# A graph layer's edge stage on one core: the batch's signal moves from a matmul to a drain of TensorE's sequencer

## Chip, core and metric

The kernel runs on 1 core of one Trainium2 chip. The metric is the device time of one execution in microseconds (us); lower is better. Before the change: 4782.93 us, the median of 3 runs (4782.77 to 4783.48). All data is float32, indices are int32.

## What is computed

One layer of a graph network with a residual: 12,500 nodes of 160 numbers (64 scalars and 32 vectors of three) and 400,000 edges sorted by their target node `dst`. Cut to what matters:

```python
h = maximum(layernorm(x), 0)                       # per node
y0 = h[:, :64] @ W_l1_0 * a / 8                    # a: one number per node
y1 = einsum('nuc,uv->nvc', h[:, 64:].reshape(n, 32, 3), W_l1_1) * a / sqrt(32)
s0, s1 = the same with W_sc0, W_sc1
w = silu(e16 @ fc_W1 / 4) @ fc_W2 / 8              # per edge: 16 -> 64 -> 192
w_a, w_b, w_c, w_d = split(w, [64, 64, 32, 32])
ys0, ys1 = y0[src], y1[src]                        # gather
mid0 = concat[w_a * ys0 * e0, w_d * (ys1 . e1) / sqrt(3)]
mid1 = concat[(w_b * ys0)[:, :, None] * e1, (w_c * e0)[:, :, None] * ys1]
z0, z1 = scatter-add of mid0, mid1 by dst, / sqrt(10)
out = x + sin(pi/8) * [s0, s1] + cos(pi/8) * [z0 @ W_l2_0, z1 @ W_l2_1] * a / sqrt(96)
```

`e0` and `e1` are the first and the other three of four numbers per edge.

## The kernel before

**Node stage** (to about 220 us). Layer norm, both linear maps, and the table `y_d` (one row of 160 numbers per node) written to DRAM.

**Edge stage.** 3125 tiles of 128 edges, in batches of four tiles: 782 batches, the last with one tile. The stage is one Python loop over `b`, fully unrolled, in an order written out by hand: under `manual_schedule` TensorE, VectorE and ScalarE run what the loop emits in the order in which it emits it. Step `b` of the loop emits, in this order:

- `weigh(b + 2)` (L574 to L584): four matmuls at L582 (eight instructions on TensorE, as each float32 matmul runs as two) turn the hidden layer `hT` into the batch's 192 edge weights per edge, in one of two PSUM tiles `pw`; then ScalarE copies three numbers per edge into the same tile (L583). The next matmuls into a `pw` tile wait until VectorE has made the products of the batch two earlier.
- `name_rows(b + 10)` (L545): ScalarE copies the batch's gather indices, `ids`.
- What earlier steps left for ScalarE (`leaving`): `hT` from the hidden matmul (L571), sums out of PSUM (`zs` L629, `za` L641, `os` L654 and L655).
- `lift_rows(b + 2)` (L493): ScalarE scales the four gathered rows of 160 by `e0`.
- `dots_of(b + 1)` (L498 to L501) and `products(b + 1)` (L505, L506, L509, L510) on VectorE, which read `pw`, the gathered rows `yg` and the lifted rows. L510 is the last reader of `pw`. Every third step `select` (L600) makes the one-hot matrices of the next three batches from the target indices.
- `load(b + 10)` (L555): GpSimd issues four indirect DMAs, one for each tile, that gather rows of `y_d` by `src`. Nine `yg` buffers lie between this and its use. 22 of the batches do not gather: their rows are made on the spot out of kept rows of `x` ("made" rows: transposes at L709 and matmuls at L720 to L722 on TensorE, 88 times each).
- `accumulate` (L665, L668): VectorE adds a finished group of nodes into the result.
- `sums(b)` (L623): four matmuls (eight instructions) multiply the one-hot matrices with the products and add them up in PSUM tile `pz` over the tiles of a group of nodes; at a group's end `turn` (three transposes, L637) and `map_sums` (three matmuls, L650) follow a few steps later.
- On even steps `hidden` (L566): one matmul (two instructions) into `px`, the hidden layer of the batches ahead.

SyncE loads edge features `xe` (L277) ten batches ahead, each load waiting for the matmuls that read its buffer before.

**Signals of TensorE.** TensorE signals on one semaphore, and in each batch the last weights matmul does it, for all matmuls since the signal before. In the built program 781 of the 782 batches have this signal; 99 hidden matmuls, 80 of the sums, 16 transposes and 4 maps of the stage signal as well. ScalarE waits for the batch's signal before L583, in an instruction of its sequencer that also waits for VectorE. What ScalarE reads from PSUM later in the step was finished before the weights and needs no wait of its own. VectorE's L498 waits for L583 (ScalarE's semaphore) and for the batch's gathers, and through L583 for the weights.

Of the kernel before, what the change touches and what calls it, by code (L numbers as in the profile page):

```python
# [18 lines left out]
P = 128  # L19
M0 = 64  # L20
M1 = 32
D = M0 + 3 * M1
FC_IN = 16
FC_H = 64
NW = 2 * M0 + 2 * M1
# [5 lines left out]
TG = 12  # L31
# [14 lines left out]
def kernel(  # L46
# [19 lines left out]
    nc = tc.nc  # L66
    N = x.shape[0]
    NT = attr.shape[1]
# [49 lines left out]
    ident = const.tile([P, P], F32, name="ident")  # L118
# [93 lines left out]
    wn0 = const.tile([P, 2, M0], F32, name="wn0")  # L212
    wn1 = const.tile([P, 2, 3 * M1], F32, name="wn1")

    w1 = const.tile([P, 2 * FC_H], F32, name="w1")
    w2 = const.tile([P, NW], F32, name="w2")

    wo = const.tile([P, 3, D], F32, name="wo")
    wc = const.tile([P, 3, D], F32, name="wc")
# [70 lines left out]
    a_sb = const.tile([P, NT], F32, name="a_sb")  # L290
# [23 lines left out]
    with (  # L314
# [129 lines left out]
        with tc.manual_schedule(engines=engines):  # L444
# [11 lines left out]
            last = len(steps) - 1  # L456
# [57 lines left out]
    with (  # L514
# [13 lines left out]
        pxs = [banks.tile([P, 512], F32, name=f"px{i}") for i in range(2)]  # L528
        turns = {"px": 0}

        def next_px():
            turns["px"] += 1
            return pxs[turns["px"] % 2]
# [4 lines left out]
        def tiles_of(b):  # L538
            return list(range(b * GT, min((b + 1) * GT, T)))
# [20 lines left out]
        def hidden(s):  # L560

            if 2 * s < NB:
                xe = blocks[s * 2 * GT // BT]
                r = slice(32 * (s % 4), 32 * (s % 4 + 1))
                ph = next_px()
                nc.tensor.matmul(ph, w1[r, :], xe[r, :], start=True, stop=True)  # L566
                leaving.append(lambda: activate(s, ph))

        def activate(s, ph):
            hT = hid.tile([P, 512], F32, name="hT")  # L570
            nc.scalar.activation(hT, ph, AF.Silu, scale=1.0 / math.sqrt(FC_IN))  # L571
            hids[s] = hT

        def weigh(b):  # L574
            hT = hids[b // 2]
            pw = pws[b % 2]
            n = len(tiles_of(b))
            for k in (0, 2, 1, 3):
                if k < n:
                    r = slice(FC_H * (k // 2), FC_H * (k // 2 + 1))  # L580
                    o = P * (b % 2 * 2 + k % 2)
                    nc.tensor.matmul(pw[:, k, 0:NW], hT[r, o:o + P], w2[r, :], start=True, stop=True)  # L582
            nc.scalar.activation(pw[:, :n, NW:NW + 3], e4_of(b)[:, :n, 1:4], AF.Copy)  # L583
            wts[b] = pw  # L584

# [4 lines left out]
        def e4_of(b):  # L590
            g, k = divmod(b, K)
            o = g % EG * TG + k * GT
            return raws[g // EG][:, o:o + GT, :]
# [22 lines left out]
        def sums(b):  # L616
            pr = prs.pop(b)
            for k, t in enumerate(tiles_of(b)):
                g = group_at[t]
                first, last = t == starts[g], t == ends[g] - 1  # L620
                if first:
                    z_ps[g] = pzs[g % 2][:, 0:ZC]
                nc.tensor.matmul(z_ps[g], sels[t // TG][:, t % TG, :], pr[:, k, :], start=first, stop=last)  # L623
                if last:
                    leaving.append(lambda g=g: z_out(g))

        def z_out(g):
            zs = post.tile([P, ZC], F32, name="zs")
            nc.scalar.activation(zs, z_ps.pop(g), AF.Copy)  # L629
            z_sb[g] = zs  # L630

        def turn(g):

            zs = z_sb.pop(g)
            pt = pzs[g % 2][:, 0:3 * P].rearrange("p (k c) -> p k c", k=3)
            for k in range(3):
                nc.tensor.transpose(pt[:, k, :], zs[:, P * k:P * (k + 1)], ident)  # L637

            def out_of():
                za = post.tile([P, 3, P], F32, name="za")  # L640
                nc.scalar.activation(za, pt, AF.Copy)  # L641
                zT[g] = za
            leaving.append(out_of)

        def map_sums(g):

            za = zT.pop(g)
            px = next_px()
            for k, lo, hi in ((0, 0, 96), (2, 96, D), (1, M0, D)):
                nc.tensor.matmul(px[:, lo:hi], za[:, k, :], wc[:, k, lo:hi], start=k == 0, stop=k == 1)  # L650

            def out_of():
                os = post.tile([P, 1, D], F32, name="os")
                nc.scalar.activation(os[:, 0, 0:M0], px[:, 0:M0], AF.Copy)  # L654
                nc.scalar.activation(os[:, 0, M0:].rearrange("p (u c) -> p c u", c=3),  # L655
                                     px[:, M0:D].rearrange("p (c u) -> p c u", c=3), AF.Copy)
                o_sb[g] = os
            leaving.append(out_of)
# [46 lines left out]
        def made_turn(r, k):  # L705
            hm, oh = turned.pop((r, k))
            pt = next_px()[:, 0:3 * P].rearrange("p (k c) -> p k c", k=3)
            for i, v in enumerate((hm[:, 0:P], hm[:, LO:D], oh)):
                nc.tensor.transpose(pt[:, i, :], v, ident)  # L709

            def out_of():
                tm = mk.tile([P, 3, P], F32, name="m_t")
                nc.scalar.activation(tm, pt, AF.Copy)
                turned[r, k] = tm
            leaving.append(out_of)

        def made_map(r, k):
            tm = turned.pop((r, k))
            po = next_px()
            nc.tensor.matmul(po[:, 0:M0], tm[:, 0, :], wn0[:, 0, :], start=True, stop=True)  # L720
            nc.tensor.matmul(po[:, M0:D], tm[:, 1, :], wn1[:, 0, :], start=True, stop=True)
            nc.tensor.matmul(po[:, D:D + NT], tm[:, 2, :], a_sb, start=True, stop=True)  # L722

            def out_of():
                pm = mk.tile([P, D + NT], F32, name="m_p")
                nc.scalar.activation(pm, po[:, 0:D + NT], AF.Copy)
                mapped[r, k] = pm
            leaving.append(out_of)
# [13 lines left out]
        def plan(r):  # L742

            b = made_at[r]
            step, lag = (6, 2) if b * GT <= wide else (12, 6)
            end = b - 7 - lag
            last = end - (end + 1) % 6
            first = last - step * (GT - 1)
            for when, b, f in ([(at_start, first - 6, made_load), (on_vector, first - 3, made_moments),
                                (on_vector, first - 1, made_reciprocal)]):  # L750
                when.setdefault(max(b, 0), []).append(lambda f=f: f(r))
            for k in range(GT):
                j = first + step * k
                for when, b, f in ((on_vector, j - 1, made_rows), (on_tensor, j, made_turn), (on_tensor, j + lag, made_map),
                                   (on_vector, j + lag + 2, made_attr), (on_scalar, j + lag + 3, made_leave)):
                    when.setdefault(b, []).append(lambda f=f, k=k: f(r, k))
# [15 lines left out]
        with order:  # L772
# [6 lines left out]
            for s in range(3):  # L779
                hidden(s)  # L780
                all_leave()
# [4 lines left out]
            for b in range(min(2, NB)):  # L786
                weigh(b)
                lift_rows(b)
# [7 lines left out]
            for g, e in enumerate(last_batch):  # L796
                at_end = e + 4 >= NB
                t = e + (1 if at_end else 2)
# [4 lines left out]
            for b in range(NB + 3):  # L803
                u, k = divmod(b, K)
# [3 lines left out]
                if b < NB:  # L808
                    q, r = divmod(b, EG * K)
# [6 lines left out]
                if b + 2 < NB:  # L816
                    weigh(b + 2)
# [17 lines left out]
                if b < NB:  # L835
                    sums(b)
                for g in turns_at.get(b, []):
                    turn(g)
                for g in maps_at.get(b, []):
                    map_sums(g)  # L840
                if b % 2 == 0:
                    hidden((b + 6) // 2)
# [5 lines left out]
    with (  # L848
# [11 lines left out]
        with tc.For_i(0, n, 1) as _:  # L860
# [4 lines left out]
            with tc.For_i(0, TP // GT, 1) as g:  # L865
                xe = fp.tile([FC_IN, 512], F32, name="f_xe")
# [30 lines left out]
                pr = fp.tile([P, GT, ZC], F32, name="f_pr")  # L897
# [3 lines left out]
                for k in range(GT):  # L901
# [16 lines left out]
                    zs = fp.tile([P, ZC], F32, name="f_zs")  # L918
# [4 lines left out]
            with tc.For_i(0, NT, 1) as i:  # L923
                zt = fp.tile([P, ZC], F32, name="f_zt")
                nc.sync.dma_start(zt, z_d[ds(i * P, P), :])
                pt = fpp.tile([P, 3, P], F32, name="f_pt")
# [4 lines left out]
                po = fpp.tile([P, D], F32, name="f_po")  # L931
# [50 lines left out]
```

## Time and profile before

| | |
|---|---|
| median of 3 runs | 4782.93 us |
| the profiled execution's own time | 4772.01 us |
| its span (first to last instruction) | 4770.2 us |
| mean granted TensorE clock | 0.904 |
| VectorE busy | 3410.0 us (71%) |
| GpSimd busy | 2967.2 us (62%) |
| ScalarE busy | 1819.5 us (38%) |

How to read it: all numbers on the profile come from the one profiled execution. PE is TensorE's matmuls, PEld its weight loads, DVE VectorE, ACT ScalarE, POOL GpSimd, SP SyncE; a "q" behind an engine is its sequencer, which waits, signals and issues DMAs and is not counted as busy. A matmul's end is modelled by the profile, its start is recorded. In a view by time a row is: start (us), duration (us), engine, line, operation, out<-in, shapes, how many were merged, and in brackets the engine's idle time before it and what ended that. A row of the waits is: engine, its tile and line <- what it waited for: us in total, times, longest. In the view of one line a row is: engine, operation, count: shortest/median/longest ns, first and last start in us. "issue" and "remote" are waits whose end the profile cannot put down to an engine.

### The profile page before, as it was taken

The numbers are of one execution on the slowest core, as the hardware profiler recorded it, in microseconds if no ns is written. First come the engines' busy times: TensorE is split into PE (matmuls) and PEld (weight loads), VectorE is DVE, ScalarE is ACT, GpSimd is POOL, SyncE is SP. The second block draws the span as 40 slices with busy tenths as digits, with TensorE's granted clock in tenths as the row PEclk, the third lists the DMA queues.
The fourth block names the chain that finished last, engine by engine and source line by source line (L and its number), as shares of the span: only waits on it lengthen the run. The fifth ranks groups of instructions, "written<-read, shape, count | busy, mean of one in ns | idle before, by whom it ended". The sixth has DMA issues, their size and how long they took to land.

```text
span 4770.2 us, 55691 instructions
## 1 busy us (share of the span) xinstructions
PE 4061.2 (85%) x16329; PEld 2320.6 (49%) x16329; DVE 3410.0 (71%) x7531; ACT 1819.5 (38%) x6330; POOL 2967.2 (62%) x3137
## 2 busy tenths in 40 slices
PE   3568988888888888888888888998988889889988
PEld 3434554444454445444444445555545445555544
DVE  4547777777777777777777767777777777777766
ACT  3423334333343333333433333333333434343333
POOL 4466666666666666666666666666666666666663
PEclk7779899899999998999998899898989998898988
DMA  5422222222222222222222222222222222232222
GB/s 175 136 61 65 65 67 66 61 65 65 67 66 65 67 65 63 64 65 68 67 64 68 63 63 63 64 66 62 67 62 63 66 63 68 62 105 63 62 61 61
DMA packets 227725, 333.87 MB, mean 70 GB/s; under 512 B 54714, under 2 KB 171526, under 8 KB 227158
## 3 DMA queue, kind: packets, MB, share of 16 engines
q0 software_dynamic: 150000, 256.20, 21.8%
q1 hardware_dynamic: 63618, 65.63, 4.4%
q10 hardware_dynamic: 13796, 8.44, 0.6%
q8 instruction: 129, 2.11, 0.2%
q14 instruction: 182, 1.49, 0.1%
HBM read 306.83 MB, written 23.22 MB: 69 GB/s over the span
## 4 chain that ended last, share of the span: by engine, by line
PE 25%; another core or an unknown queue 23%; issue 22%; DVE 18%; ACT 10%; DMA 1%; ACTq 0%; DVEq 0%; POOL 0%; SPq 0%; POOLq 0%
PE pz L623 15%; PE pw L582 6%; ACT yge L493 5%; DVE pr L506 3%; DVE tmp L498 3%; DVE tmp L501 2%; PE px L566 2%; DVE pr L510 2%; DVE pr L509 2%; DVE both L500 2%; ACT pw L583 1%; DVE pr L505 1%; DVE sel L600 1%; ACT hT L571 1%
## 5 line engine op out<-in xcount | busy, mean ns | idle before, releaser
L555 POOL DMA_INDIRECT yg<-y_d,ids x2997 | 2842.2, 948 | 1612.5 <-issue 782.1
L623 PE MATMUL pz<-pr,sel 128*128 128x384 f32 x6250 | 2529.9, 549 | 143.5 <-issue 83.9
L623 PEld LDWEIGHTS pz<-pr,sel 128*128 128x128 f32 x6250 | 1253.0, 211 | 1130.3 <-issue 550.7
L498 DVE TENSOR_TENSOR tmp<-yg,pw 128x384 f32<-128x384 f32 x760 | 416.7, 548 | 1147.5 <-ACT pw L583 1084.6
L583 ACT ACTIVATE pw<-raw 128x12 f32<-128x12 f32 x782 | 139.8, 179 | 2802.8 <-issue 1190.0
L582 PE MATMUL pw<-w,hT 64*128 64x192 f32 x6250 | 825.8, 368 | 388.6 <-DVE pr L510 238.9
L493 ACT ACTIVATE yge<-yg,raw 128x160 f32<-128x160 f32 x3037 | 1044.9, 421 | 0.0
L582 PEld LDWEIGHTS pw<-w,hT 64*128 64x128 f32 x6250 | 546.8, 196 | 780.5 <-issue 416.3
L506 DVE TENSOR_TENSOR pr<-both,pw 128x768 f32<-128x768 f32 x782 | 736.9, 942 | 0.0
L566 PE MATMUL px<-xe,w 32*128 32x512 f32 x782 | 444.2, 650 | 35.2 <-ACT hT L571 20.4
L600 DVE TENSOR_TENSOR sel<-pw,drel 128x1536 f32<-128x1536 f32 (+1 forms) x261 | 454.8, 1743 | 0.0
L501 DVE TENSOR_REDUCE tmp<-tmp 128x128 f32<-128x384 f32 x782 | 454.7, 581 | 0.0
L510 DVE TENSOR_TENSOR pr<-pw,yge 128x384 f32<-128x384 f32 x782 | 426.3, 545 | 0.0
L509 DVE TENSOR_TENSOR pr<-pw,yge 128x256 f32<-128x256 f32 x782 | 325.5, 416 | 6.5 <-ACT yge L493 6.5
L500 DVE TENSOR_TENSOR both<-pw,yg 128x256 f32<-128x256 f32 x760 | 316.0, 416 | 0.0
L505 DVE TENSOR_TENSOR pr<-pw,tmp 128x128 f32<-128x128 f32 x782 | 224.4, 287 | 18.0
L566 PEld LDWEIGHTS px<-xe,w 32*128 32x128 f32 x782 | 115.2, 184 | 240.1 <-issue 152.3
L571 ACT ACTIVATE hT<-px 128x512 f32<-128x512 f32 x391 | 228.0, 583 | 2.0 <-PE px L566 1.7
L650 PEld LDWEIGHTS px<-wc,za 128*128 128x128 f32 x1110 | 152.1, 196 | 49.7 <-issue 8.6
L650 PE MATMUL px<-wc,za 128*128 128x96 f32 x1110 | 153.4, 275 | 6.1 <-ACT za L641 4.6
L668 DVE SCALAR_TENSOR_TENSOR acc<-os,by,acc 128x160 f32 x370 | 143.4, 388 | 14.4 <-ACT os L655 1.0
L545 ACT ACTIVATE ids<-src_sb 128x4 int32<-128x4 int32 x750 | 143.0, 191 | 0.2
(120 smaller groups left out, 1773.5 us busy)
## 6 DMA issues: line engine op xcount, KB each, us to landing
yg<-y_d,ids POOLq DMA_INDIRECT x2997
xe<-in_e SPq DMA_DIRECT2D x196, 128.0 KB
y_d<-ys ACTq DMA_DIRECT2D x12, 640.0 KB
xr_d<-xr SPq DMA_DIRECT2D x22, 320.5 KB
acc<-in_x SPq DMA_DIRECT2D x11, 640.0 KB
xm<-xr_d SPq DMA_DIRECT2D x22, 320.0 KB
out<-acc SPq DMA_DIRECT2D x11, 640.0 KB
raw<-in_e SPq DMA_DIRECT2D x32, 192.0 KB
```

The source lines that it names most:

```text
L493: nc.scalar.activation(yge[:, k, :], yg[:, k, :], AF.Copy, scale=e4v[:, k, 0:1])
L498: nc.vector.tensor_tensor(tmp[:, :n, 0:3, :], y1, wt[:, :n, NW:NW + 3].unsqueeze(3).to_broadcast([P, n, 3, M1]), ALU.mult)
L500: nc.vector.tensor_mul(both[:, :n, :], wt[:, :n, 96:160], yg[:, :n, 0:M0])
L501: nc.vector.tensor_reduce(tmp[:, :n, 3, :], tmp[:, :n, 0:3, :].rearrange("p t c u -> p t u c"), AX.X, ALU.add)
L506: nc.vector.tensor_mul(pr[:, :n, 192:ZC].rearrange("p t (c u) -> p t c u", c=3), both[:, :n, :].unsqueeze(2).to_broadcast([P, n, 3, M0]), ...
L509: nc.vector.tensor_mul(pr[:, :n, 0:M0], wt[:, :n, 0:M0], yge[:, :n, 0:M0])
L510: nc.vector.tensor_mul(pr[:, :n, 96:192].rearrange("p t (c u) -> p t c u", c=3), wt[:, :n, M0:96].unsqueeze(2).to_broadcast([P, n, 3, M1]) ...
L555: nc.gpsimd.indirect_dma_start(out=yg[:, k, :], out_offset=None, in_=y_d, in_offset=bass.IndirectOffsetOnAxis(ap=ids[b][:, k:k + 1] if b i ...
L566: nc.tensor.matmul(ph, w1[r, :], xe[r, :], start=True, stop=True)
L582: nc.tensor.matmul(pw[:, k, 0:NW], hT[r, o:o + P], w2[r, :], start=True, stop=True)
L600: nc.vector.tensor_tensor(sels[u][:, 0:n, :].rearrange("p t (k c) -> p t k c", k=GT), for_each, drel[:, u * TG:u * TG + n].unsqueeze(2).un ...
L623: nc.tensor.matmul(z_ps[g], sels[t // TG][:, t % TG, :], pr[:, k, :], start=first, stop=last)
```

## The change

Behind the weights matmuls of each batch stands a drain of TensorE's sequencer, and the drain is declared to stand for all matmuls since the drain before it. The matmuls of the stage are collected in a group (`on_pe`); an instruction that depends on one of them waits for the drain that closes the group.

```diff
+        behind = {"drain": 0}
+
+        def on_pe(ins):
+            tc.add_to_no_dep_group(f"pe{behind['drain']}", ins.ins)
+
+        def drained():
+            tc.declare_fence(nc.tensor.drain().ins, group=f"pe{behind['drain']}")
+            behind["drain"] += 1
...
-                nc.tensor.matmul(ph, w1[r, :], xe[r, :], start=True, stop=True)
+                on_pe(nc.tensor.matmul(ph, w1[r, :], xe[r, :], start=True, stop=True))
...
-                    nc.tensor.matmul(pw[:, k, 0:NW], hT[r, o:o + P], w2[r, :], start=True, stop=True)
+                    on_pe(nc.tensor.matmul(pw[:, k, 0:NW], hT[r, o:o + P], w2[r, :], start=True, stop=True))
+            drained()
             nc.scalar.activation(pw[:, :n, NW:NW + 3], e4_of(b)[:, :n, 1:4], AF.Copy)
...
-                nc.tensor.matmul(z_ps[g], sels[t // TG][:, t % TG, :], pr[:, k, :], start=first, stop=last)
+                on_pe(nc.tensor.matmul(z_ps[g], sels[t // TG][:, t % TG, :], pr[:, k, :], start=first, stop=last))
```

`turn`, `map_sums`, `made_turn` and `made_map` are wrapped in `on_pe` in the same way.

In the built programs the order of all other instructions is the same on every engine. TensorE has 782 drains more, each with a signal; no weights matmul signals any longer, and of the other matmuls of the stage 11 do (the first ones and the last ones). ScalarE waits for the drain where it waited for the matmul. VectorE's L498 waits for the drain as well, beside L583 and the gathers, and has one semaphore instruction more for it in 780 batches. SyncE's 96 loads of `xe` wait for a drain where they waited for a matmul.

More of the change, by code (lines that the diff above doesn't have):

```diff
@@ L636, in turn @@
             for k in range(3):
-                nc.tensor.transpose(pt[:, k, :], zs[:, P * k:P * (k + 1)], ident)
+                on_pe(nc.tensor.transpose(pt[:, k, :], zs[:, P * k:P * (k + 1)], ident))
             def out_of():
@@ L649, in map_sums @@
             for k, lo, hi in ((0, 0, 96), (2, 96, D), (1, M0, D)):
-                nc.tensor.matmul(px[:, lo:hi], za[:, k, :], wc[:, k, lo:hi], start=k == 0, stop=k == 1)
+                on_pe(nc.tensor.matmul(px[:, lo:hi], za[:, k, :], wc[:, k, lo:hi], start=k == 0, stop=k == 1))
             def out_of():
@@ L708, in made_turn @@
             for i, v in enumerate((hm[:, 0:P], hm[:, LO:D], oh)):
-                nc.tensor.transpose(pt[:, i, :], v, ident)
+                on_pe(nc.tensor.transpose(pt[:, i, :], v, ident))
             def out_of():
@@ L719, in made_map @@
             po = next_px()
-            nc.tensor.matmul(po[:, 0:M0], tm[:, 0, :], wn0[:, 0, :], start=True, stop=True)
-            nc.tensor.matmul(po[:, M0:D], tm[:, 1, :], wn1[:, 0, :], start=True, stop=True)
-            nc.tensor.matmul(po[:, D:D + NT], tm[:, 2, :], a_sb, start=True, stop=True)
+            on_pe(nc.tensor.matmul(po[:, 0:M0], tm[:, 0, :], wn0[:, 0, :], start=True, stop=True))
+            on_pe(nc.tensor.matmul(po[:, M0:D], tm[:, 1, :], wn1[:, 0, :], start=True, stop=True))
+            on_pe(nc.tensor.matmul(po[:, D:D + NT], tm[:, 2, :], a_sb, start=True, stop=True))
             def out_of():
```

## The prediction

> **What bounds the kernel now.** I read the page's busy table and clock first, then the waits, then one stretch in order of time, then the rows of each engine that could become the bound.
>
> ```profile
> span 4770.2 us, 55691 instructions
> ...
> PE 4061.2 (85%) x16329; PEld 2320.6 (49%) x16329; DVE 3410.0 (71%) x7531; ACT 1819.5 (38%) x6330; POOL 2967.2 (62%) x3137
> ...
> PEclk7779899899999998999998899898989998898988
> ...
> PE 25%; another core or an unknown queue 23%; issue 22%; DVE 18%; ACT 10%; DMA 1%; ACTq 0%; DVEq 0%; POOL 0%; SPq 0%; POOLq 0%
> ```
>
> No engine is full, and 45% of the chain that ended last has no owner ("unknown queue" and "issue"). The waits say in front of which line that time lies:
>
> ```profile
> ACT pw L583 <- issue: 1190.0, 275, 36.5
> ACT pw L583 <- remote: 1160.4, 126, 11.1
> DVE tmp L498 <- ACT pw L583: 1098.5, 246, 34.7
> ...
> PE pw L582 <- DVE pr L510: 238.9, 155, 10.6
> ...
> PE pw L582 <- issue: 123.3, 171, 3.8
> ```
>
> ScalarE idles 2350 us before L583 (1190.0 + 1160.4), the small copy that follows each batch's weights; VectorE then idles 1098.5 us for L583. L583 waits for the signal on the last weights matmul. So I asked whether that signal is on time. Up to 2405 us the two lines have run this often:
>
> ```profile
> L582 PE MATMUL pw<-w,hT x3016: 319/323/687, 224.4 to 2403.8; 64*128 64x192 f32 x189
> ```
>
> ```profile
> L583 ACT ACTIVATE pw<-raw x376: 160/183/185, 226.1 to 2398.5; 128x12 f32<-128x12 f32 x188
> ```
>
> A batch has eight weights matmuls, so TensorE has finished 377 batches of them and ScalarE has run L583 for 376: the weights from 2403.16 us are those for which ScalarE waits next. What follows, in order of time:
>
> ```profile
> 2403.16 0.92 PE L582 MATMUL pw<-w,hT 64*128 64x192 f32 x8
> ...
> 2404.01 2.85 PE L623 MATMUL pz<-pr,sel 128*128 128x384 f32 x8
> ...
> 2407.84 0.92 PE L582 MATMUL pw<-w,hT 64*128 64x192 f32 x8
> ...
> 2410.05 0.19 PEld L623 LDWEIGHTS pz<-pr,sel 128*128 128x128 f32 x1 [0.42 <-issue]
> 2410.76 1.45 PE L623 MATMUL pz<-pr,sel 128*128 128x384 f32 x4 [0.51 <-issue]
> ...
> 2410.90 0.18 ACT L583 ACTIVATE pw<-raw 128x12 f32<-128x12 f32 x1 [10.32 <-issue]
> ...
> 2411.12 0.55 DVE L498 TENSOR_TENSOR tmp<-yg,pw 128x384 f32<-128x384 f32 x1 [4.43 <-ACT pw L583]
> ```
>
> The weights end at 2404.08 us; L583 starts at 2410.90, 6.8 us later, with ScalarE idle all the while, and VectorE starved for 4.43 us. TensorE worked on meanwhile, even through the next batch's weights, and L583 was released only after TensorE's stream broke (0.70 us between the load at 2410.05 and its matmul). The sequencer's wait before it is the 10690 ns here:
>
> ```profile
> L583 ACTq EVENT_SEMAPHORE  x3: 38/1583/10690, 2396.9 to 2411.2; - x3
> ```
>
> It can hardly be the other half of that wait, VectorE's release of the bank, since TensorE's matmul into that bank needed it too. Against it, a batch for which TensorE had waited idle:
>
> ```profile
> 2043.80 0.63 PEld L582 LDWEIGHTS pw<-w,hT 64*128 64x128 f32 x8 [0.76 <-DVE m_oh L702]
> 2043.80 0.92 PE L582 MATMUL pw<-w,hT 64*128 64x192 f32 x8
> ...
> 2044.82 0.18 ACT L583 ACTIVATE pw<-raw 128x12 f32<-128x12 f32 x1 [1.20 <-issue]
> ```
>
> Here L583 starts 0.10 us after the weights' end (2044.72). My reading: a matmul's signal is seen late, by microseconds, when TensorE's stream behind it is dense, and on time when it is not. VectorE starves, then TensorE waits for VectorE, and the engines take turns instead of overlapping. The stage runs from the first weights (224.4 us, in the counts above) to the last:
>
> ```profile
> 4751.28 0.59 PE L582 MATMUL pw<-w,hT 64*128 64x192 f32 x2
> ```
>
> That is 4526.9 us for 782 batches, 5.79 us each. The profiled execution took 4772.0 us, so 245.1 lie outside the stage; it is 10.9 us below the median of the runs, which I add at the end.
>
> **The change, part by part.** *The signal moves* from the last weights matmul to a drain behind it. I take a drain as ending when TensorE is empty and as holding back what stands behind it, so that nothing is dense behind the signal. I take the wait before L583 to fall to the 0.10 us above. What does each engine then need per batch? For TensorE, four steps in which it did not wait, at a granted clock of 1.00:
>
> ```profile
> 2016.83 0.92 PE L582 MATMUL pw<-w,hT 64*128 64x192 f32 x8 [1.49 <-issue]
> ...
> 2021.51 0.92 PE L582 MATMUL pw<-w,hT 64*128 64x192 f32 x8
> ...
> 2025.05 0.49 PE L637 MATMUL pz<-ident,zs 128*128 128x128 f32 x3
> 2025.38 0.33 PE L720 MATMUL px<-wn,m_t 128*128 128x64 f32 x2
> ...
> 2026.11 0.92 PE L582 MATMUL pw<-w,hT 64*128 64x192 f32 x8
> ...
> 2030.79 0.92 PE L582 MATMUL pw<-w,hT 64*128 64x192 f32 x8
> ...
> 2034.33 0.81 PE L650 MATMUL px<-wc,za 128*128 128x96 f32 x6
> 2035.06 0.76 PE L582 MATMUL pw<-w,hT 64*128 64x192 f32 x6
> ```
>
> ```profile
> 2016.50:2035.50 19.00, 18.67 (x89) 11.21 (x91) 16.41 (x36) 6.51 (x23) 12.19 (x14) 1.00 0.22 54
> ...
> 360.00:4700.00 4340.00, 3813.43 (x15171) 2152.46 (x15171) 3189.75 (x6874) 1664.19 (x5901) 2772.03 (x2924) 0.92 0.26 66
> ```
>
> Steps with a hidden-layer matmul take 4.68 us; one with a group's L650 4.27; the one with L637 takes 4.60, of which 0.7 belongs to work on rows made on the spot (L720 to 2026.11), rare (88 such steps), so some 3.9 without. That gives (4.68 + 4.1) / 2 = 4.39, plus 0.12 for the made rows (88 steps each with the 0.73 us of L720 to L722 and with three transposes like L637's 0.33 us: 93 / 782), **4.51 us**.
>
> *Each drain costs TensorE* the time from the next batch's work starting early to its starting late. Today L623 starts 0.07 us before the weights end (4.01 against 4.08); that overlap goes. The trace has no drain inside a stream; at the program's end an idle engine's drain takes 8 ns on TensorE and up to 174 on ScalarE:
>
> ```profile
> L978 PEldq DRAIN  x2: 8/8/8, 4763.9 to 4769.7; - x2
> L978 ACTq DRAIN  x2: 8/91/174, 4765.1 to 4769.7; - x2
> ```
>
> Low end 0.07 + 0.01 = 0.08 us. High end 0.07 + 0.17 + one slow start of 0.70 (the broken stream above) = 0.94. A gain in this term I exclude: a drain does no work. I take 0.25, nearer the low end, because nothing in the steps above starts as late as the broken stream did. All of it lies on the path wherever TensorE sets the pace.
>
> The Trainium skill ("TensorE: Matmul & The Clock Gate", "What happens when you issue a matmul") speaks against drains: the array's run-out, normally under the next matmul, is exposed when nothing follows, about 175 ns. As an estimate from that page the sum below would be 59 us shorter with 0.175 for 0.25; no run here shows it.
>
> *The clock.* 0.92 over the stage, 1.00 where TensorE ran unbroken. With fewer long idles I take 0.975: 4.51 / 0.975 adds 0.12 us (bounds 0 and 0.39).
>
> *VectorE* gets one semaphore instruction more per batch before L498, which now waits for the drain itself:
>
> ```profile
> L498 DVEq EVENT_SEMAPHORE  x1519: 21/50/50, 222.0 to 4753.1; - x190
> ```
>
> At 0.05 us it is covered by L583's 0.18 us, for which L498 waits anyway; uncovered it costs at most 782 x 0.05 = 39 us. Behind it stand VectorE's seven products of the batch, and TensorE's sums for them. VectorE's work is 3189.75 us in 4340 of the stage, 4.26 us per batch of 5.79: below TensorE's. The loads of edge features on SP wait for the drain in place of a matmul and run many batches ahead.
>
> *GpSimd* becomes a close second bound. Its gathers leave 1.25 us apart when nothing holds them:
>
> ```profile
> L555 POOL DMA_INDIRECT yg<-y_d,ids x2997: 941/947/1098, 266.7 to 4720.1; - x200
> ```
>
> ```profile
> 2400.11 0.95 POOL L555 DMA_INDIRECT yg<-y_d,ids  x1 [0.30 <-issue]
> 2401.36 0.95 POOL L555 DMA_INDIRECT yg<-y_d,ids  x1 [0.30 <-issue]
> ```
>
> 2997 x 1.25 = 3746 us, with the 40 first ones (another line of the same view) 3796 at most: 4.79 to 4.85 us per batch.
>
> *The sum.* TensorE 4.51 + 0.25 + 0.12 = 4.88 us, GpSimd 4.79, VectorE 4.26. Steps are uneven and only two banks of weights lie between the engines, so some waiting stays: today's wait of TensorE for VectorE is 238.9 / 782 = 0.31 us; I keep a third, 0.10. So 4.98 x 782 = 3894 us; with the 245 outside 4139, and 10.9 to the median: **4150 us**, 13% faster. With every bound low, GpSimd's 3796 rules: 4052.
>
> **Rivals.** *The drain is dear* (0.94 us, its high end): 4.51 + 0.94 + 0.12 + 0.10 = 5.67 us, 4434, 4690 in all. For it: starts 0.70 us apart exist. Against: they appear where the stream broke, not after each wait. It would stop paying at a drain of 5.79 - 4.73 = 1.06 us.
>
> *The signals were on time and ScalarE waited for something else.* Then only the drain's price is new: about 450 of 782 batches had no TensorE wait before L582 (326 in the two rows) to hide 0.25 us in, 113 us: 4896, slower. Against it: the 10.32 us with the bank already free. The Trainium skill ("PSUM — Partial Sum Buffer", "Engine vs sequencer instructions") has this rule: a signal on the matmul fires on completion and is the place for it; a drain waits until the engine is fully idle. The 2403.16 us batch disagrees by 6.8 us.
>
> *The end itself comes late, not its report,* so that the drain holds TensorE as long as L583 was held. The wait of 2350 us would then lie in TensorE's stream, less its present idle before L582 and L623 of about 530: 4783 + 1820 = 6600. It decides once drains average 1.06 us. Against it: VectorE reads those banks only after L583, and the next batch's matmuls went on at full pace.
>
> *The change does not do what it says*: signals stay late for a cause that a drain leaves alone, and the drain hides in TensorE's idle: within 0.2% of 4783.
>
> **How the numbers follow.** Forecast 0.72 (4052 to 4360, the last with the clock left at 0.92), dear drain 0.12, on-time signals 0.08, late ends 0.04, no effect 0.02, and 0.02 for less than the forecast's low end. Faster by over 0.2%, about what a measurement here can tell, 0.86 (forecast, dear drain and the last); within 0.2% 0.02; slower 0.12. The range runs from 4020, between the two counts of gathers, to 4470, a drain of 0.66 us, and leaves out half of the dear drain and the slower cases.
>
> **What would show it.** L583's idle of 2350 us (the two largest rows) shrinks to well under half, with no 10 us wait of its sequencer; drains stand in TensorE's queue 782 times, each from the weights' end; the first L623 starts about 0.25 us after that end; steps without waits take some 4.8 us; gathers stand 1.25 us apart nearly throughout; the clock rises over 0.92. Wrong would be: drains that average over 1 us, L583 late by microseconds after them, or L498 waiting for gathers.

## The result, and the profile after

| | before | after |
|---|---|---|
| median (us), four runs each | 4783.2 | 5120.14 |
| lowest to highest | 4782.77 to 4790.52 | 5105.29 to 5121.9 |
| ratio, 95% interval | | 1.069 (1.067 to 1.072): slower |
| profiled execution, its span | 4772.01, 4770.2 | 5118.6, 5116.8 |
| mean granted TensorE clock | 0.904 | 0.880 |

The page of the kernel after, its busy table, clock row and chain:

```profile
span 5116.8 us, 57253 instructions
...
PE 4132.3 (81%) x16329; PEld 2353.0 (46%) x16329; DVE 3448.6 (67%) x7531; ACT 1845.2 (36%) x6330; POOL 2959.9 (58%) x3137
...
PEclk7789898899898889888889889988988898988889
...
PE 79%; issue 17%; another core or an unknown queue 2%; DVE 1%; ACT 1%; DMA 1%; PEldq 0%; POOL 0%; DVEq 0%; ACTq 0%; PEld 0%; SPq 0%
```

TensorE now owns the chain that ended last (79%, before 25%), but not because it works more. Its busy time rose by 71.1 us (4061.2 to 4132.3) and its idle time by 275.5 (709.0 to 984.5, span less busy). Together that is the 346.6 us by which the span grew. Where the idle time lies, by groups, before and after:

```profile
L623 PE MATMUL pz<-pr,sel 128*128 128x384 f32 x6250 | 2529.9, 549 | 143.5 <-issue 83.9 <-ACT za L641 57.5
L582 PE MATMUL pw<-w,hT 64*128 64x192 f32 x6250 | 825.8, 368 | 388.6 <-DVE pr L510 238.9 <-issue 123.3 <-DVE by L665 23.1
```

```profile
L633 PE MATMUL pz<-pr,sel 128*128 128x384 f32 x6250 | 2681.5, 581 | 846.1 <-issue 805.7
L591 PE MATMUL pw<-w,hT 64*128 64x192 f32 x6250 | 722.6, 350 | 3.8 <-DVE pr L510 3.7
```

(L623, L582 and L583 of before are L633, L591 and L593 of after; the drain is L537.) TensorE's idle time in front of the weights fell from 388.6 to 3.8 us; of the waits for VectorE's L510 in it, 238.9 us, the forecast kept a third, and 3.7 are left. In front of the sums, right behind the drain, 143.5 became 846.1. The waits of after:

```profile
ACT pw L593 <- PEq L537: 2863.0, 671, 34.8
PEld pz L633 <- issue: 1438.7, 2011, 29.1
DVE tmp L498 <- ACT pw L593: 1166.3, 530, 33.0
POOL yg L564 <- ACT ids L554: 1117.5, 456, 9.1
```

ScalarE's wait did not fall from 2350 us; the profile can now name what ends it, the drain, and it is 2863.0. A late batch and a prompt one, in order of time:

```profile
2391.81 0.94 POOL L564 DMA_INDIRECT yg<-y_d,ids  x1 [2.29 <-ACT ids L554]
...
2399.75 0.92 PE L591 MATMUL pw<-w,hT 64*128 64x192 f32 x8
...
2400.56 0.95 POOL L564 DMA_INDIRECT yg<-y_d,ids  x1 [0.30 <-issue]
...
2403.25 4.54 PE L633 MATMUL pz<-pr,sel 128*128 128x384 f32 x8 [2.58 <-issue]
2403.31 0.18 ACT L593 ACTIVATE pw<-raw 128x12 f32<-128x12 f32 x1 [5.18 <-PEq L537]
...
2403.89 0.94 POOL L564 DMA_INDIRECT yg<-y_d,ids  x1 [2.38 <-ACT ids L554]
...
2407.64 0.95 POOL L564 DMA_INDIRECT yg<-y_d,ids  x1 [0.30 <-issue]
...
2408.77 0.92 PE L591 MATMUL pw<-w,hT 64*128 64x192 f32 x8
...
2409.78 1.55 PE L633 MATMUL pz<-pr,sel 128*128 128x384 f32 x4
2409.84 0.18 ACT L593 ACTIVATE pw<-raw 128x12 f32<-128x12 f32 x1 [4.30 <-PEq L537]
```

The weights at 2408.77 end at 2409.69; the sums start 0.09 us later and L593 0.15: the drain is as cheap as forecast. The weights at 2399.75 end, as the profile models it, at 2400.67. TensorE then stands for 2.58 us, and its eight sums take 4.54 us where 2.84 is normal, since the granted clock has dropped. The busy time of these stretches (start:end, length, PE busy, clock, DMA share, GB/s), behind the late drain and behind the prompt one:

```profile
2403.20:2405.80 2.60, 2.55 (x5) 0.59 0.11 26
2409.70:2411.50 1.80, 1.72 (x6) 1.00 0.04 10
```

Between 2401.5 and 2403.2 no engine works; all that is under way is rows of the last gather, whose last packet ends at 2402.77. Now the GpSimd rows: before the late batch eight gathers had started without a break (2391.81 to 2400.56); before the prompt one four (2403.89 to 2407.64).

The kernel before shows the same in the two batches that the prediction compared, if GpSimd's rows are put beside them:

```profile
2395.10 0.95 POOL L555 DMA_INDIRECT yg<-y_d,ids  x1 [0.30 <-issue]
...
2407.62 0.95 POOL L555 DMA_INDIRECT yg<-y_d,ids  x1 [0.30 <-issue]
2413.50 0.95 POOL L555 DMA_INDIRECT yg<-y_d,ids  x1 [4.92 <-ACT ids L545]
```

```profile
2040.10 0.95 POOL L555 DMA_INDIRECT yg<-y_d,ids  x1 [2.89 <-ACT ids L545]
...
2043.85 0.94 POOL L555 DMA_INDIRECT yg<-y_d,ids  x1 [0.30 <-DVE m_oh L702]
```

The weights of 2403.16, whose L583 came 6.8 us late at 2410.90, fell into a run of at least eleven gathers, and L583 came 3.3 us after the start of its last one. The weights of 2043.80, prompt, fell on the fourth gather behind a pause.

So the theory after the result, G: **while a run of GpSimd's gathers is in flight, TensorE's end of work is reported late, whether by a matmul's signal or by a drain.** Before, TensorE ran on past a late signal; with the drain it stands.

Over 748 batches (the 21st to the 768th; late means that L593, or L583, starts over 0.6 us after both the modelled end of its weights and ScalarE's own last instruction; a run is a row of gathers at most 1.5 us apart; where the last gather started over 2.65 us before, the run counts as over):

| gathers of the run started by the weights' end | none to 4 | 5 or 6 | 7 and more | all late; their median (us) | lateness of all 748 ends, sum (us) |
|---|---|---|---|---|---|
| before: late of all | 25 of 265 | 58 of 114 | 228 of 369 | 311; 5.85 | 1694 |
| after: late of all | 64 of 506 | 5 of 5 | 237 of 237 | 306; 2.66 | 827 |

Of the two sums, the late ends alone make 1675 and 759 us.

In the kernel before, 141 of the 369 ends in the longest runs do not count as late. That does not make their signals prompt: in 140 of the 141, L583 came more than 0.6 us after the weights (4.60 us in the median), but ScalarE had only just finished other work, so this trace cannot tell whether the signal was there before. In the kernel after, the 242 ends behind six or more gathers are let go when the run is over: the sums start 2.70 us after the start of the last gather in the median, and between 2.66 and 2.76 us in half of the cases.

### The profile page after: what moved, and what is told of

Same layout as the page of the kernel before. It is cut to its first block, busy times and chain, and to the rows that moved or that the text cites. A ratio compares the mean times of both kernels' runs of the same rounds, so it can differ in the third digit from the quotient of the medians.

```text
span 5116.8 us, 57253 instructions
## 1 busy us (share of the span) xinstructions
PE 4132.3 (81%) x16329; PEld 2353.0 (46%) x16329; DVE 3448.6 (67%) x7531; ACT 1845.2 (36%) x6330; POOL 2959.9 (58%) x3137
## 4 chain that ended last, share of the span: by engine, by line
PE 79%; issue 17%; another core or an unknown queue 2%; DVE 1%; ACT 1%; DMA 1%; PEldq 0%; POOL 0%; DVEq 0%; ACTq 0%; PEld 0%; SPq 0%
PE pz L633 52%; PE pw L591 13%; PE px L575 8%; PE px L660 2%; PE pz L647 1%; PE px L719 1%; PE px L731 0%; PE px L732 0%; PE px L730 0%; ACT ys L433 0%; DVE st L375 0%; DVE mv L376 0%; DMA y_d<-ys 0%; DVE h L378 0%
## 5 line engine op out<-in xcount | busy, mean ns | idle before, releaser
L564 POOL DMA_INDIRECT yg<-y_d,ids x2997 | 2834.6, 946 | 1962.1 <-ACT ids L554 1117.5
L633 PE MATMUL pz<-pr,sel 128*128 128x384 f32 x6250 | 2681.5, 581 | 846.1 <-issue 805.7
L633 PEld LDWEIGHTS pz<-pr,sel 128*128 128x128 f32 x6250 | 1325.5, 223 | 1897.0 <-issue 1438.7
L498 DVE TENSOR_TENSOR tmp<-yg,pw 128x384 f32<-128x384 f32 x760 | 420.6, 553 | 1404.4 <-ACT pw L593 1143.9
L593 ACT ACTIVATE pw<-raw 128x12 f32<-128x12 f32 x782 | 143.1, 183 | 3121.0 <-PEq L537 2863.0
L591 PE MATMUL pw<-w,hT 64*128 64x192 f32 x6250 | 722.6, 350 | 3.8 <-DVE pr L510 3.7
L591 PEld LDWEIGHTS pw<-w,hT 64*128 64x128 f32 x6250 | 491.6, 186 | 357.4 <-issue 184.7
L510 DVE TENSOR_TENSOR pr<-pw,yge 128x384 f32<-128x384 f32 x782 | 428.5, 548 | 0.0
L554 ACT ACTIVATE ids<-src_sb 128x4 int32<-128x4 int32 x750 | 141.6, 189 | 0.6
```

What stands on the lines that cost most here:

```text
L498: nc.vector.tensor_tensor(tmp[:, :n, 0:3, :], y1, wt[:, :n, NW:NW + 3].unsqueeze(3).to_broadcast([P, n, 3, M1]), ALU.mult)
L510: nc.vector.tensor_mul(pr[:, :n, 96:192].rearrange("p t (c u) -> p t c u", c=3), wt[:, :n, M0:96].unsqueeze(2).to_broadcast([P, n, 3, M1]) ...
L564: nc.gpsimd.indirect_dma_start(out=yg[:, k, :], out_offset=None, in_=y_d, in_offset=bass.IndirectOffsetOnAxis(ap=ids[b][:, k:k + 1] if b i ...
L591: on_pe(nc.tensor.matmul(pw[:, k, 0:NW], hT[r, o:o + P], w2[r, :], start=True, stop=True))
L633: on_pe(nc.tensor.matmul(z_ps[g], sels[t // TG][:, t % TG, :], pr[:, k, :], start=first, stop=last))
```

## Experiments

Each time stands beside one of the kernel before on the same chip, which turned out to matter. "Hold" is short for TensorE's late ends; the column says whether the chip is of the kind that shows them, on which the kernel before takes about 4800 us.

| run | us | before, same chip | hold | late of 748 |
|---|---|---|---|---|
| E1 drain, no gathers | 3906.29 | 4836.4 | yes | 0 |
| E2 signal, no gathers | 3783.87 | 4836.4 | yes | 0 |
| E3 drain, SyncE's plain loads | 3904.14 | 4836.4 | yes | 0 |
| E4 signal and bare drain | 5129.4 | 4836.4 | yes | 285 |
| E5 drain, GpSimd's fills | 3797.96 | 3971.52 | no | 0 |
| E6, E10 drain, GpSimd's plain loads | 3797.62, 3798.49 | 3971.52, 3963.55 | no | 0 |
| E14 the same | 3913.62 | 4825.25 | yes | 0 |
| E7, E11 drain, free gathers | 3970.66, 3960.45 | 3971.52, 3963.55 | no | 0 |
| E13 the same | 5462.56 | 4825.25 | yes | 263 |
| E8, E12 signal, free gathers | 3972.0, 3962.43 | 3971.52, 3963.55 | no | 0 |
| E9 the changed kernel | 3962.69 | 3963.55 | no | 0 |
| E15, E17, E18 drain, rows in order | 3962.38, 3964.28, 3961.45 | 3962.68, 3963.46, 3962.84 | no | 0 |
| E16 drain, half of the gathers | 3796.21 | 3962.68 | no | 0 |

### E1 and E2: the gathers left out

```diff
             yg = ygp.tile([P, GT, D], F32, name="yg")
-            rows[b] = yg
+            rows[b] = held[b] = yg
...
+            if b >= YB:
+                rows[b] = held[b % YB]
+                return
```

> The changed kernel with the gathers of the edge stage left out: from the tenth batch on, the rows gathered for the first nine batches are read again and again, so GpSimd is idle in the stage and the sums are wrong. Theory G (TensorE's end-of-work report, drain or signal, is held back while gathers of GpSimd are in flight): no drain ends more than 0.3 us after the modelled end of its weights, TensorE is the only bound at 4.51 + 0.16 us for a prompt drain over a clock of 0.97, 4.8 us a batch, some 3990 us in all (3900 to 4150). Rival V (it is VectorE's one-hot step every third batch, or something in TensorE's own stream): about a third of the drains stays 2 us late, and the time stays at 4900 to 5120.

> The kernel before with the same gathers left out. Theory G: the signals on the weights matmuls come on time too, L583's idle of 2350 us falls below 800, and the time lies within 150 us of the changed kernel without gathers, shorter than it by the prompt drain's own price, 0.16 us x 782 = 125 us: 3870 us or so. Rival D (a matmul's signal is late because TensorE's stream behind it is dense, as predicted): signals stay late by microseconds and the time stays above 4600.

G's times came in: 3906.3 us, and 3783.9 where some 3870 were expected, with no late end in either. The groups of E1 (its L636 is the sums), then a stretch of E2:

```profile
L636 PE MATMUL pz<-pr,sel 128*128 128x384 f32 x6250 | 2224.8, 499 | 99.3 <-issue 28.7
```

```profile
2400.31 0.92 PE L585 MATMUL pw<-w,hT 64*128 64x192 f32 x8
...
2401.16 2.85 PE L626 MATMUL pz<-pr,sel 128*128 128x384 f32 x8
2401.33 0.18 ACT L586 ACTIVATE pw<-raw 128x12 f32<-128x12 f32 x1 [3.18 <-issue]
```

In E2 the sums start before the weights end (2401.16 against 2401.23), so TensorE's stream is as dense as it can be, and the signal is seen 0.10 us after the end. That refutes the prediction's reason, the dense stream. One number of G's missed: idle before L586 is still 1673 us in E2, where less than 800 was expected. ScalarE there waits for work, not for a report: idle time of an engine that is not the bound proved nothing. The difference of the two is the prompt drain's price: 122.4 us / 782 = 0.157 us a batch.

### E3: the same bytes as plain loads

```diff
+                for k, t in enumerate(tiles_of(b)):
+                    nc.sync.dma_start(yg[:, k, :], y_d[t % 97 * P:(t % 97 + 1) * P, :])
+                return
```

> The changed kernel with each gather replaced by a plain load of 128 whole rows of the same table into the same place, issued by SyncE: the same bytes into SBUF, but no descriptors written by GpSimd (the rows are the wrong ones). Theory G with GpSimd's descriptors as cause: drains prompt, 3900 to 4200 us. Rival M (any transfer into SBUF holds the report back): a third of the drains stays 2 us late, 4900 us or more.

3904.1 us, as without any load, though SyncE's queue now moves the gathers' bytes:

```profile
q1 hardware_dynamic: 495762, 311.66, 29.6%
...
L637 PE MATMUL pz<-pr,sel 128*128 128x384 f32 x6250 | 2223.7, 499 | 99.0 <-issue 28.3
```

Transfers into SBUF as such do not hold TensorE. The Trainium skill ("SBUF — State Buffer", "Who interferes with whom") says that a DMA never contends with a compute engine and that TensorE never waits on anyone. E3 agrees; the late ends beside gathers, where the chip has the hold, do not. Whether a port of the memory has to do with them was not found.

### E4: a bare drain beside the signal

```diff
                     nc.tensor.matmul(pw[:, k, 0:NW], hT[r, o:o + P], w2[r, :], start=True, stop=True)
+            nc.tensor.drain()
```

> The kernel before, the weights' last matmul signalling as it did, with a drain behind each batch's weights that signals nothing: the hold on TensorE's stream alone, without the move of the signal. Theory H (the drain's hold is the whole loss): 5120 us within 1%, with the same third of late ends. Rival S (the move of the signal costs by itself): between 4783 and 5050. If a matmul's signal is seen late beyond the drain, L583 starts microseconds after the drain's end and the time is above 5200.

```profile
ACT pw L584 <- issue: 3104.9, 755, 33.8
...
PE pz L624 <- issue: 829.0, 332, 26.9
```

5129.4 us, 0.2% from the changed kernel, and TensorE stands 829.0 us behind the drain where after showed 805.7. On its own chip E4 is 6.1% above the kernel before, the changed kernel 6.9% on its own, so nearly all of the loss is the hold of TensorE's stream. What the move of the signal adds, or saves, is about 1% at most; single runs on two chips cannot say more. In E4, 39 of 502 ends with up to four gathers started are late, and 246 of 246 with six or more.

### E9: another chip, another result

E5 to E8 ran where the kernel before took 3971.5 us, so the changed kernel was run again as it is:

> The changed kernel once more, as it is, because the kernel before took 3971.5 us on the chip of the last four runs and 4836.4 on that of the first four. Theory C (the hold on TensorE's ends is there on some chips only; where it isn't, GpSimd's gathers bound both kernels): where the kernel before takes about 3970 us, the changed kernel takes 3965 to 4100 with prompt drains; where it takes about 4800, 5090 to 5140 with late ones. Rival N (the drain costs its 340 us on every chip): 4250 or more where the kernel before takes 3970.

3962.69 against 3963.55 us: no difference that can be measured, though TensorE drains 782 times. From its groups, its waits and its timeline:

```profile
L564 POOL DMA_INDIRECT yg<-y_d,ids x2997 | 2838.2, 947 | 913.0 <-issue 739.0
L633 PE MATMUL pz<-pr,sel 128*128 128x384 f32 x6250 | 2244.2, 503 | 72.6 <-DVE by L675 1.5
```

```profile
ACT yge L493 <- DMA yg<-y_d,ids: 730.4, 841, 4.0
DVE tmp L498 <- DMA yg<-y_d,ids: 352.6, 298, 4.3
```

```profile
2400.15 0.92 PE L591 MATMUL pw<-w,hT 64*128 64x192 f32 x8
2400.64 0.95 POOL L564 DMA_INDIRECT yg<-y_d,ids  x1 [0.30 <-issue]
...
2401.16 2.84 PE L633 MATMUL pz<-pr,sel 128*128 128x384 f32 x8
2401.22 0.18 ACT L593 ACTIVATE pw<-raw 128x12 f32<-128x12 f32 x1 [2.32 <-PEq L537]
```

Here all 748 ends fall behind nine gathers or more of an unbroken run, and none is late (L593 0.15 us after the weights at 2400.15 end). The unbroken run is not what makes them prompt: the fourth batch of the stage fell behind 27 gathers of a run in the kernel after, and its L593 came 28.8 us late; in E9 it fell behind 21 and came 0.15 us after the weights. GpSimd is the bound: its gathers stand 1.25 us apart, ScalarE and VectorE wait for gathered rows, and the drain's 0.157 us fits into TensorE's slack. Theory C holds, and G needs a condition: on some chips.

### E7, E11, E13: gathers that wait for no index copy

```diff
-                if b + AHEAD < NB:
-                    name_rows(b + AHEAD)
```

> The changed kernel without the copies of the indices: each gather reads its row numbers from the whole table of them, so it waits for its buffer alone and no longer for the small copy behind the drain. Gathers then leave 1.25 us apart nearly throughout. Theory P (an end is held until the gathers in flight pause, so an unbroken run holds longer): drains late by more than the 2.55 us of today, time above 5200 us. Rival E (an end is held only where a run of gathers breaks off, the drains that fell into a longer run having been prompt): hardly a late drain, and the time follows GpSimd's 3746 us of gathers and TensorE's 4.8 us a batch: 4000 to 4250 us.

> The changed kernel without the copies of the indices again; where the kernel before takes 3970 us, 3971 as before. On a chip where it takes about 4800: theory P (an end is held until the gathers in flight pause, so an unbroken run holds longer) above 5200 us; rival E (an end is held only where a run of gathers breaks off) 4000 to 4250 us.

> The changed kernel without the copies of the indices, a third time: on two chips the hold on TensorE's ends did not occur (3971 and 3960 us, the kernel before 3972 and 3964), and nothing new is expected there. On a chip where the kernel before takes about 4800 us: theory P (an end is held until the gathers in flight pause, so an unbroken run holds longer) above 5200 us; rival E (an end is held only where a run of gathers breaks off) 4000 to 4250 us.

The first two ran without the hold and tell nothing of it; GpSimd's pace is the same with or without its leash. E13 ran with the hold and bears out theory P: 5462.6 us. A stretch of it:

```profile
2401.98 0.95 POOL L564 DMA_INDIRECT yg<-y_d,src_sb  x1 [2.28 <-ACT yge L493]
...
2408.00 0.92 PE L591 MATMUL pw<-w,hT 64*128 64x192 f32 x8
...
2410.74 0.94 POOL L564 DMA_INDIRECT yg<-y_d,src_sb  x1 [0.30 <-issue]
2412.02 4.33 PE L633 MATMUL pz<-pr,sel 128*128 128x384 f32 x8 [3.10 <-issue]
2412.08 0.18 ACT L593 ACTIVATE pw<-raw 128x12 f32<-128x12 f32 x1 [5.79 <-PEq L537]
```

A run of eight gathers, and TensorE waits 3.10 us until it is nearly through. In E13, 40 of 506 ends with up to four gathers are late, 11 of 26 with five, 212 of 216 with six or more; the median late one is 3.61 us, against 2.66 in the kernel after. There are fewer late ends than there (263 against 306), but they last longer. The leash, the copy that starts a batch's gathers only behind its weights, keeps the runs short on such a chip: past the first batches the longest run of after is eight gathers, while 59 of E13's are of twelve.

> The kernel before, likewise without the copies of the indices. Theory P: signals seen later than now, 4783 us or more, up to 5200. Rival E: signals on time, 3950 to 4150 us, GpSimd's gathers being the bound.

> The kernel before without the copies of the indices again; where the kernel before takes 3970 us, 3972 as before. On a chip where it takes about 4800: theory P 4783 us or more, up to 5200; rival E 3950 to 4150 us.

E8 and E12 had no chip with the hold; what free gathers do to the kernel before there was not seen.

### E5, E6, E10, E14: GpSimd's work and its plain loads

```diff
+            if b >= YB + 1:
+                nc.gpsimd.tensor_copy(yg[:, 0, 0:GT], ids[b])
+                for k, t in enumerate(tiles_of(b)):
+                    nc.gpsimd.dma_start(yg[:, k, :], y_d[t % 97 * P:(t % 97 + 1) * P, :])
+                return
```

E5 has six fills `nc.gpsimd.memset(yg, 0.0)` in place of the loads.

> The changed kernel with each batch's four gathers replaced, from the eleventh batch on, by GpSimd's own work of about the same length and at the same place: a copy that waits for the batch's indices and six fills of the same buffer with zeros (so the sums are wrong), and no transfer at all. Theory T (what holds TensorE's end back is a transfer that GpSimd started, on its way): drains prompt, 3900 to 4100 us. Rival W (GpSimd at work, writing to SBUF, is enough): a third of the drains ends 2 us late, 4900 us or more.

> The changed kernel with each gather replaced, from the eleventh batch on, by a plain load of 128 whole rows of the table into the same place, issued by GpSimd, behind a small copy that waits for the batch's indices as the gathers did (wrong rows). Theory T with any transfer whose descriptors GpSimd writes: late drains stay, 4700 to 5200 us. Rival R (only the gather by row numbers does it): drains prompt, 3900 to 4100 us, as with SyncE's plain loads (3904).

> GpSimd's plain loads in place of the gathers again, meant for a chip on which the kernel before takes about 4800 us; where it takes 3970, nothing new is expected (3798). Theory T with any transfer whose descriptors GpSimd writes: late drains stay, 4700 to 5200 us. Rival R (only the gather by row numbers does it): drains prompt, 3900 to 4000 us.

> GpSimd's plain loads in place of the gathers, a third time: 3798 us where the kernel before takes 3970 or less. On a chip where it takes about 4800: theory T with any transfer whose descriptors GpSimd writes, late drains stay, 4700 to 5200 us; rival R (only the gather by row numbers does it), drains prompt, 3880 to 3950 us.

E5, E6 and E10 ran without the hold and show only TensorE's own pace, 3798 us; whether GpSimd's own work, without a transfer, holds TensorE's ends was thus not tested. E14 ran with it, beside E13, and has no late end:

```profile
L638 PE MATMUL pz<-pr,sel 128*128 128x384 f32 x6250 | 2225.2, 499 | 104.2 <-issue 33.6
L566 POOL DMA_DIRECT2D yg<-y_d x2997 | 1592.5, 537 | 903.6 <-ACT yge L493 559.9 <-DVE tmp L498 120.8 <-issue 104.1
```

This is rival R's number. Of E14's ends 64 fell behind six or more loads of a run, and none was late, where gathers held 242 of 242 in the kernel after. But these loads take 537 ns each, not 947, so a run of as many is over sooner, and gathers too held few ends in short runs. That plain loads by GpSimd never hold is not shown.

### E15 to E18: scattered rows, and half of the gathers

```diff
-                nc.scalar.activation(ids[b][:, :n], src_sb[:, b * GT:b * GT + n], AF.Copy)
+                nc.scalar.activation(ids[b][:, :n], lane_i[:, :n], AF.Copy)
```

> The changed kernel with the same 3000 gathers by row numbers, paced as they are, but the numbers are 0 to 127 in order for every tile of the batches from the eleventh on (wrong rows). On a chip where the kernel before takes about 4800 us: theory I (the gather instruction by itself holds TensorE's ends back) 5050 to 5150 us with about 300 late ends; rival S (it is the scattered rows of the table that do it, as GpSimd's plain loads read rows in order) prompt ends and GpSimd's bound, 3960 to 4120 us. Where the kernel before takes about 3970: 3960 to 3975, nothing told.

> The gathers of rows 0 to 127 in order once more; 3962 us, as before, where the kernel before takes about 3970. On a chip where it takes about 4800: theory I (the gather instruction by itself holds TensorE's ends back) 5050 to 5150 us with about 300 late ends; rival S (the scattered rows of the table do it) prompt ends and 3960 to 4120 us.

> The gathers of rows 0 to 127 in order, a third time; 3962 to 3964 us, as before, where the kernel before takes about 3970. On a chip where it takes about 4800: theory I (the gather instruction by itself holds TensorE's ends back) 5050 to 5150 us with about 300 late ends; rival S (the scattered rows of the table do it) prompt ends and 3960 to 4120 us.

```diff
             for k, t in enumerate(tiles_of(b)):
+                if k % 2 and b > YB:
+                    nc.sync.dma_start(yg[:, k, :], y_d[t % 97 * P:(t % 97 + 1) * P, :])
+                    continue
```

> The changed kernel with two of each batch's four gathers replaced by SyncE's plain loads (wrong rows in half of the tiles), so a batch's run of gathers takes some 2.2 us and leaves TensorE's step of 4.8 us half free. On a chip where the kernel before takes about 4800 us: theory G (a hold lasts while a gather is in flight) few late ends, since the run is over before the next weights, 3900 to 4050 us. Rival K (each gather costs TensorE a fixed time, 1210 us over 2997 gathers) half of the loss stays: 4400 to 4600. Where the kernel before takes about 3970: 3790 to 3830.

All four ran without the hold. They show that the order of the rows does not set GpSimd's pace (3961 to 3964 us) and that half of the gathers leave TensorE as the bound (3796). Whether scattered rows are needed for a hold, and whether half of the gathers would end it, stays open.

## Why the prediction was wrong

**The reason for the late signal** is the step that failed: "a matmul's signal is seen late, by microseconds, when TensorE's stream behind it is dense". E2 has the dense stream and prompt signals. The late L583 was real; its cause was put down from two batches compared on TensorE and ScalarE alone. The gathers of that very stretch were quoted in the prediction, for GpSimd's pace only.

**"I take the wait before L583 to fall to the 0.10 us above"** follows from that reason and fell with it: it is nearly so (0.15 us in the batch at 2408.77) in the 442 of 748 batches of after that are not late. In the other 306 the drain ends late too, and L593 starts 2.66 us late in the median.

**The drain's own price**, 0.25 us a batch, was mis-sized by little where the end is prompt: 0.157 (E1 less E2), inside its bounds of 0.08 to 0.94. The Trainium skill's 175 ns for an exposed run-out ("TensorE: Matmul & The Clock Gate", "What happens when you issue a matmul") is near it.

**The clock** was to rise from 0.92 to 0.975 because long idles would go. They did not; over the same stretch (360 to 4700 us) the clock fell to 0.89, and the sums behind late drains, at 0.59 in the stretch above, make the longer L633 of the groups (2529.9 to 2681.5 us). Not every late drain did this: where the sums started 0.6 to 1.8 us after the weights' end (66 of the 306) their matmuls took 0.50 us each in the median, as behind prompt drains; from 2.4 us on (222) they took 0.74. Without gathers the clock of the whole span is 0.981 (E1).

With the measured sizes the prediction's sum comes out: 4.51 us at 0.89 is 5.07, and with the 1.11 that a drain costs on average here (below) and nothing kept for VectorE's banks 6.18 a batch, an estimate. The stage of the kernel after took 6.23, from its first weights at 226.7 us to its last at 5098.1.

**GpSimd as the second bound**, 3746 to 3796 us, was right, where no hold hides it: from E9's first weights (149.2) to its last (3940.1) are 3790.9 us. There the kernel before is at this bound already, and the change brings nothing, which the forecast, made from a trace with the hold, could not see.

**The rival "the end itself comes late, not its report"** named what happened, a drain that holds TensorE, and was given 0.04. Whether the end itself is late, or only a report for which a drain waits as well, no run separates. What was held against it, that "the next batch's matmuls went on at full pace", is no evidence: a stream that nothing stops runs on past a late end. Its point, drains that average over 1.06 us, was passed: 827 / 748 = 1.11 us from the weights' end to L593, with the 0.15 us of the prompt ones in it. Its 6600 us was too high because it took ScalarE's 2350 us as fixed. A late drain delays L593, the index copy behind it and so the next gathers (POOL waits 1117.5 us for L554), the run breaks off and the hold ends: 827 us late in all, where the signals of before were 1694.

**What would show it** did so: L583's idle did not shrink, L593's is late by microseconds, and the gathers do not stand 1.25 us apart nearly throughout. The drains stand in TensorE's queue 782 times, but their rows start before the weights end (by 1.38 us at least) and cannot be read as a price:

```profile
L537 PEldq DRAIN  x782: 1415/4872/36175, 225.6 to 5095.0; - x196
```

Their ends can. A drain's row ends 0.03 us after its weights in the 442 prompt batches, and 2.54 us after them in the 306 late ones (medians).

## What to carry to other kernels

A wait that ends late has a cause on some engine: before pricing the cure, compare a late and a prompt case on all engines and queues, GpSimd's too. A drain turns a late report, which costs only its readers, into a stop of the engine, which costs most where ends come late. Where they came on time the drain gained nothing either: E1 is 122 us slower than E2, and E9 is level with the kernel before. And a trace shows one chip: where a kernel's time differs by 20% between chips, a change has to be judged on both kinds.

## What the runs showed of the hardware

On the chips of the comparison of before and after, of E1 to E4 and of E13 and E14, TensorE's ends are late beside long runs of gathers; on those of the other runs never. The kernel before takes 4783 to 4836 us on the first kind and 3963 to 3972 on the second. The gathers themselves run alike on both (946 to 948 ns each, 1.25 us apart). The node stage shows what looks like the same hold, where GpSimd gathers rows of `x` (L354): TensorE's transposes (L407) wait for the copies of the transposes before them (L414). The waits of the kernel before up to 226 us, then E9's up to 150:

```profile
ACT hT L414 <- remote: 88.5, 6, 29.1
PEld pt L407 <- ACT hT L414: 74.6, 30, 29.1
```

```profile
PEld pt L407 <- ACT hT L414: 28.7, 34, 5.0
```

The longest wait is 29.1 us there and 5.0 in E9, which has no such wait of L414 for a "remote" end, and the edge stage starts at 224.4 us against 149.2. This parts the two kinds in every trace: the first weights start at 224 to 229 us in the eight with the hold and at 147 to 150 in the other twelve. Chip 7 was without the hold twice, half an hour apart (E5 to E8 and E17); no chip with the hold is known to have been seen a second time, so that it belongs to the chip, and not to the hour, is likely and not shown. What differs between the chips, why up to four gathers hold few ends and six nearly all, and which part of a gather does it, was not found. A kernel that beats both was not found either: on chips with the hold the kernel before is the fastest of those that compute the layer, and on the others all of them stand at GpSimd's bound.
